# Keeping TensorE side pieces out of the round after a VectorE read of the side PSUM bank

## The chip, the cores and the metric

The kernel runs on one NeuronCore of one Trainium2 chip. The metric is the device time of one execution, in microseconds (us). The kernel before takes 10168.11 us, the median of three runs (10168.09 to 10171.36). The five engines are TensorE (PE, with its weight loads PEld), VectorE (DVE), ScalarE (ACT), GpSimd (POOL) and SyncE (SP, which here only issues DMAs).

## The reference

Two graph layers on 3327 nodes with 128 features; `adj` is a 0/1 matrix with about 0.24% ones and a full diagonal. Layer 0 is graph attention, layer 1 is a graph transformer in which the adjacency is added to the scores twice, once as "spatial" and once as "edge" encoding. Each layer is followed by a residual and a layer norm. Cut to what is computed:

```python
# layer 0
H = x @ W.T + b;  s = H @ a_s;  r = H @ a_r
e = leaky_relu(A * s + A * r.T, negative_slope=0.2)
att = softmax(where(A > 0, e, -9e15), axis=1)
x = layernorm(x + att @ H)
# layer 1: d = 128 "heads" of n = 3327 positions with h = 8 features
q, k, v = ((x @ Wx.T).reshape(d, n, h) for Wx in (Wq, Wk, Wv))
a = einsum('dnh,dmh->dnm', q, k) * d ** -0.5 + adj + adj
out = einsum('dnm,dmh->dnh', softmax(a, axis=2), v)
x = layernorm(x + out.reshape(n, h * d) @ Wo.T)
```

Nearly all the work is in layer 1: 128 score matrices of 3327 x 3327, each with an exponential per element. Because `q`, `k` and `v` are plain reshapes, a slice of 128 rows of layer 0's result feeds only a few of the 128 heads. So layer 1 can begin when the first row tile of layer 0 is ready, and the rest of layer 0 can be computed beside it.

## The kernel before, in words

The two layers run interleaved in one long loop, inside `special()`. (`shifted()` and `general()` are run only when a test of the data's range fails; here they don't run.)

**The main loop.** 32 groups `g` of four heads, in each 7 blocks `b` of 476 query columns, in each block 26 rounds `n`: 32 x 7 x 26 = 5824 rounds. Keys are cut into 26 tiles. In a round four score matmuls (L135) fill two PSUM tiles `scb` with the scores of two (key tile, half of the heads) pairs. Every third key tile is a "times" tile: ACT takes the exponential straight from PSUM (L1007), and POOL multiplies it by a factor made of the adjacency (L1008). For the other tiles DVE adds the adjacency out of PSUM into SBUF (L1010), and ACT takes the exponential a round later, for a whole tile (L843). The products of the exponentials with the values (L813, tile `av`) follow four rounds later. Rounds come in threes: two rounds with one times half and one added half each, then one round with two added halves. The last two rounds of a block, n = 24 and 25, are of the first kind, and so are the rounds 0 and 1 of the next block. There are two PSUM buffers `scb` for the added tiles and one for the times tiles, one PSUM bank for `av`, and one PSUM bank, `bank` (pool `sx_ps`, one buffer), for all the rest.

**The side work.** The remaining 25 row tiles of layer 0, and the last projection with its layer norm (`result`), are cut into pieces and run in the gaps of the loop. There are two rows of pieces. `main` holds, for each tile, 26 products of the attention (p, on TensorE, L450), then a chain that alternates between TensorE and DVE: transpose (`turn`), copy (`keep_turned`), and for each of 24 chunks of 128 columns a projection p (`project`, L373) that writes `bank`, and a DVE piece d that reads `bank`: for 16 chunks of q and k `halves` (two instructions, L386 and L389), for 8 chunks of v `values` (one copy, L408). `result` has such pairs too (`turn` at L472, `divided` at L481). `aside` holds the attention weights and counts: d pieces on DVE (L295, L313), m pieces on POOL (L304), x pieces (loads on SP).

**Who runs when.** `lane("p", n)` lets one p of `main` run in the rounds n = 3, 4, 7, 10, 13, 16, 19, 22, 24 and 25; `lane("d", n)` one d in 0, 4, 7, ..., 22, 24 and 25. A p is issued by `work_tensor` right after the round's score matmuls and ahead of its products. The d, from `main` if its head is a d and else from `aside`, is issued by `work` at the end of the round, behind the round's additions. The order is fixed when the program is built; every engine then works through its own list in order, held by semaphores. A p takes a new tile from the one-buffer pool `sx_ps`, so it waits until DVE is done with the piece before.

**The deadline.** 28 rounds before a group ends (L980) `finish_to` forces all pieces of `main` that the next group's rows still need, one after the other, into the program at that place. If they are done by then, it adds nothing.

Of the kernel before, what the change touches and what calls it, by code (L numbers as in the profile page):

```python
# [47 lines left out]
def kernel(  # L48
# [95 lines left out]
    def special():  # L144
        with ExitStack() as sx, tc.manual_schedule(engines=ALL):
# [468 lines left out]
            with ExitStack() as st:  # L614
# [8 lines left out]
                for p0, p1 in _cut(FP):  # L623
# [8 lines left out]
                loads, main, aside = layer0(  # L632
                    0, side=False, trow=trs[0], bank=lambda: pps.tile([P, 512], F32, tag="mm", name="mm")
                )
# [224 lines left out]
            def lane(kind, n):  # L859
                middle = n % 3 == 1 and 4 <= n < NR - 2  # L860
                if kind == "p":
                    return int(middle or n == 3 or n >= NR - 2)
                return int(middle or n == 0 or n >= NR - 2)
# [3 lines left out]
            main = []  # L867
            aside = []
# [21 lines left out]
            aside.append(("t", ("counts", 0)))  # L890
            results = [((needs[t] + 1) * total + LAG + 6, result(t)) for t in range(NT)]
            marks = {("P", q): 0 for q in range(len(CH))}
            side = {"main": [], "aside": aside, "since": {"main": 0, "aside": 0}}

            def head(row, now, force=False):

                while True:
                    if not side[row]:
                        if row == "aside":
                            return None  # L900
                        ahead = ("rows", reads[min(max(now, 0) // total + 2, NG - 1)]) in marks
                        if results and results[0][0] <= now and (ahead or not main):
                            side[row] = results.pop(0)[1]
                        elif main:
                            side[row] = main.pop(0)
                        else:
                            return None
                    kind, f = side[row][0]
                    if kind == "t":
                        marks[f] = now  # L910
                    elif kind == "w":
                        if not force and now - side["since"][row] < f:
                            return None
                    elif kind == "n":
                        if f[:2] not in marks or not force and now - marks[f[:2]] < f[2]:
                            return None
                    else:
                        return kind
                    side[row].pop(0)

            def run(row, now):
                side[row].pop(0)[1]()
                side["since"][row] = now

            def work_tensor(now, n):
                for _ in range(lane("p", n)):
                    if head("main", now) != "p":
                        break
                    run("main", now)

            def work(now, n):
                room, pool = lane("d", n), 1
                for row in ("main", "aside"):
                    while True:
                        kind = head(row, now)
                        if kind == "x":
                            pass
                        elif kind == "d" and room:
                            room -= 1
                        elif kind == "m" and pool:  # L940
                            pool -= 1
                        else:
                            break
                        run(row, now)
# [22 lines left out]
            for g in range(NG):  # L967
                k4, v4, _ = group
                for b in range(NBLK):
                    s = Block()  # L970
                    s.g, s.b, s.q4, s.k4, s.v4, s.left, s.e, added = g, b, queries[0], k4, v4, NT, {}, {}
                    for n, rnd in enumerate(rounds):
# [20 lines left out]
                        for i, h in rnd:  # L993
                            sc.append((pe if i in times else pd).tile([P, 2, 512], F32, name="scb"))
                            for t in range(2):
                                scores(sc[-1][: kr[i], t, :WB], s.k4, s.q4, i, kr[i], 2 * h + t, WB)
                        work_tensor(g * total + at, n)
                        for (i, h), z in zip(rnd, sc):
                            r = kr[i]
# [11 lines left out]
                        now = g * total + at  # L1011
# [14 lines left out]
                        while len(waiting) > LAG:  # L1026
                            products(*waiting.pop(0))
                        work(g * total + at, n)
            exp_late(NG * total + 2)
            while waiting:  # L1030
# [130 lines left out]
    def general():  # L1161
        with ExitStack() as gx:
# [168 lines left out]
            with ExitStack() as pc:  # L1331
                wp = pc.enter_context(tc.tile_pool(name="pc_w", bufs=3))
                ps = pc.enter_context(tc.tile_pool(name="pc_ps", bufs=4, space=bass.MemoryType.PSUM))
                for t in range(NT):
# [30 lines left out]
                    nc.scalar.dma_start(out[t * P : t * P + r, :], y[:r])  # L1365

    special()
    fine = nc.values_load(flag[0:1, 0:1])
    with tc.If(fine < 1):
# [41 lines left out]
```

## Time and profile before

| | |
|---|---|
| Median of three runs | 10168.11 us |
| The profiled execution: its own time | 10167.89 us |
| Its span, first to last instruction | 10166.1 us |
| Mean granted TensorE clock | 0.995 |
| Busy: PE / DVE / ACT / POOL | 98% / 92% / 98% / 91% |
| Rounds, and time per block of 26 rounds | 5824, 44.5 us |

Busy time is the union of an engine's instructions. In a row of a wait view the engine and line that waited stand first, then whom it waited for, the total in us, the number of times and the longest. In a timeline the columns are start, duration, engine, line, operation, tiles with their shapes and, in brackets, the engine's idle time before it and what ended it.

### The profile page before, as it was taken

The numbers are of one execution on the slowest core, as the hardware profiler recorded it, in microseconds if no ns is written. First come the engines' busy times: TensorE is split into PE (matmuls) and PEld (weight loads), VectorE is DVE, ScalarE is ACT, GpSimd is POOL, SyncE is SP. The second block draws the span as 40 slices with busy tenths as digits, with TensorE's granted clock in tenths as the row PEclk, the third lists the DMA queues.
The fourth block names the chain that finished last, engine by engine and source line by source line (L and its number), as shares of the span: only waits on it lengthen the run. The fifth ranks groups of instructions, "written<-read, shape, count | busy, mean of one in ns | idle before, by whom it ended". The sixth has DMA issues, their size and how long they took to land.

```text
span 10166.1 us, 212027 instructions
## 1 busy us (share of the span) xinstructions
PE 9930.1 (98%) x81993; PEld 3841.6 (38%) x81993; DVE 9374.0 (92%) x11597; ACT 9981.3 (98%) x8311; POOL 9215.6 (91%) x4395
## 2 busy tenths in 40 slices
PE   7999999999999999999999999999999999999998
PEld 3333333333333333333333333333333333333333
DVE  6999999999989999999999999999999999999887
ACT  6999999999999999999999999999999999999998
POOL 6999999999989999999999999999999999998887
PEclk8999999999999999999999999999999999999999
DMA  6655555555555555555555565555665555655554
GB/s 175 202 176 167 174 172 174 173 173 167 176 166 170 177 165 173 176 167 170 168 170 178 172 179 167 156 175 173 178 177 160 164 174 176 176 153 171 165 158 125
DMA packets 1183195, 1730.00 MB, mean 170 GB/s; under 512 B 131326, under 2 KB 1170783, under 8 KB 1177949
## 3 DMA queue, kind: packets, MB, share of 16 engines
q1 hardware_dynamic: 1180810, 1714.81, 56.8%
q8 instruction: 645, 10.57, 0.4%
q14 instruction: 377, 3.09, 0.1%
q10 hardware_dynamic: 1363, 1.53, 0.1%
HBM read 1611.93 MB, written 103.95 MB: 169 GB/s over the span
## 4 chain that ended last, share of the span: by engine, by line
PE 79%; ACT 10%; DVE 5%; POOL 2%; issue 2%; DMA 1%; SPq 0%; DVEq 0%; POOLq 0%; ACTq 0%
PE av L813 41%; PE scb L135 33%; ACT e L1007 5%; ACT e L843 5%; PE bank L224 4%; DVE e L1010 3%; POOL e L1008 2%; DVE o L822 1%; DMA at<-in_adjT_dram 0%; PE bank L472 0%; DMA k4b<-kT 0%; DMA at<-ftd 0%; POOL at L803 0%; DVE lo L389 0%; DVE ot L481 0%
## 5 line engine op out<-in xcount | busy, mean ns | idle before, releaser
L1008 POOL TENSOR_TENSOR e<-e,at 128x952 f32<-128x952 f32 x4032 | 8972.4, 2237 | 836.0 <-ACT e L1007 772.8
L1010 DVE TENSOR_TENSOR e<-scb,at 128x952 f32<-128x952 f32 (+1 forms) x7616 | 8420.3, 1145 | 671.2 <-PE scb L135 365.6
L843 ACT ACTIVATE e<-e 128x1904 f32<-128x1904 f32 (+2 forms) x4256 | 6885.4, 1624 | 14.7 <-DVE e L1010 14.3
L813 PE MATMUL av<-e,v4b 128*32 128x476 f32 x46592 | 5876.9, 572 | 40.2 <-DVE o L822 28.2
L135 PE MATMUL scb<-q4b,k4b 32*128 32x476 f32 (+1 forms) x23296 | 4338.4, 592 | 121.0 <-ACT e L1007 54.0
L135 PEld LDWEIGHTS scb<-q4b,k4b 32*128 32x128 f32 (+1 forms) x23296 | 2518.9, 295 | 4796.6 <-issue 2640.6
L1007 ACT ACTIVATE e<-scb 128x952 f32<-128x952 f32 x4032 | 3881.2, 963 | 88.0 <-PE scb L135 59.4
L813 PEld LDWEIGHTS av<-e,v4b 128*32 128x32 f32 x46592 | 1058.7, 108 | 1066.5 <-issue 621.5
L224 PE MATMUL bank<-hsb,w 128*32 128x129 f32 (+1 forms) x5200 | 277.9, 285 | 0.0
L313 DVE TENSOR_SCALAR_CACHE_REDUCE dump<-a 128x384 bf16<-128x384 f32 (+2 forms) x468 | 247.4, 529 | 0.6
L295 DVE TENSOR_SCALAR w<-trow,er 128x129 f32<-128x129 f32 x650 | 201.4, 339 | 13.1 <-DMA trow<-td 13.1
L304 POOL TENSOR_TENSOR w<-w,a 128x384 f32<-128x384 f32 (+3 forms) x225 | 207.0, 920 | 0.1
L224 PEld LDWEIGHTS bank<-hsb,w 128*32 128x32 f32 (+1 forms) x5200 | 102.4, 108 | 148.4 <-issue 148.4
L822 DVE COPY o<-av 128x476 f32<-128x476 f32 x224 | 145.9, 651 | 7.9 <-PE av L813 6.9
L389 DVE SCALAR_TENSOR_TENSOR lo<-bank,hi 128x128 fp32r<-128x128 f32 (+1 forms) x400 | 116.6, 292 | 13.9
L386 DVE TENSOR_SCALAR hi<-bank 128x128 fp32r<-128x128 f32 (+1 forms) x400 | 112.3, 281 | 0.0
L224 PE MATMUL bank<-wk,x1T 128*32 128x128 f32 x1600 | 85.2, 284 | 10.7 <-DVE lo L389 10.7
L224 PE MATMUL bank<-wq,x1T 128*32 128x128 f32 x1600 | 85.2, 284 | 9.0 <-DVE lo L389 9.0
L224 PE MATMUL bank<-wv,x1T 128*32 128x128 f32 x1600 | 85.4, 285 | 5.0 <-DVE vb L408 4.0
L224 PE MATMUL bank<-wo,ot 128*32 128x128 f32 (+1 forms) x1664 | 88.8, 290 | 0.4 <-DVE ot L481 0.4
L472 PE MATMUL bank<-identr,o 128*128 128x128 f32 (+1 forms) x234 | 54.6, 308 | 15.0 <-DMA o<-oT 8.1
L408 DVE COPY vb<-bank 128x128 f32<-128x128 f32 (+1 forms) x200 | 56.2, 281 | 3.5 <-PE bank L224 3.5
(110 smaller groups left out, 665.6 us busy)
## 6 DMA issues: line engine op xcount, KB each, us to landing
at<-in_adjT_dram SPq DMA_DIRECT2D x1736, 476.0 KB
at<-ftd SPq DMA_DIRECT2D x1953, 238.0 KB
q4b<-qT SPq DMA_DIRECT2D x1788, 29.8 KB
k4b<-kT SPq DMA_DIRECT2D x126, 415.9 KB
at<-in_adjT_dram SPq DMA_DIRECT2D x217, 208.2 KB
at<-in_adjT_dram SPq DMA_DIRECT2D x56, 714.0 KB
a<-in_adjT_dram SPq DMA_DIRECT2D x50, 504.0 KB
ftd<-at SPq DMA_DIRECT2D x63, 238.0 KB
```

Source lines behind the costliest of these rows:

```text
L135: nc.tensor.matmul(dst, k4[32 * j : 32 * j + H4, i::NT], q4[32 * j : 32 * j + H4, :nb], start=True, stop=stop,)
L224: nc.tensor.matmul(dst[c0:c1], w[:, c0:c1], mov, **kw)
L295: nc.vector.tensor_scalar(w, s["t"][:, :, :T3], e, None, op0=ALU.max)
L304: nc.gpsimd.tensor_tensor(w, w, s["a"][n][:, c0 - i0 : c1 - i0, :r], op=ALU.mult)
L313: nc.vector.tensor_scalar(z, a, float(k), None, op0=ALU.is_equal, op1=ALU.add, accum_out=even[:, t, at : at + 1])
L389: nc.vector.scalar_tensor_tensor(lo[:r, o : o + QW], s["b"][:r, :QW], scale, hi[:r, o : o + QW].bitcast(F32), op0=ALU.mult, op1=ALU.subtract,)
L813: nc.tensor.matmul(s.av[32 * j : 32 * j + 32, :], s.v4[:r, j, i * H1 : i * H1 + 32], e[:r, j, :], start=(s.left == NT - 1), stop=(s.left = ...
L822: nc.vector.tensor_copy(o4, s.av)
L843: nc.scalar.activation(e, e, AF.Exp, scale=2.0)
L1007: nc.scalar.activation(eh, z[:r, :, :WB], AF.Exp, scale=2.0)
L1008: nc.gpsimd.tensor_tensor(eh, eh, ah, op=ALU.mult)
L1010: nc.vector.tensor_tensor(eh, z[:r, :, :WB], ah, op=ALU.add)
```

## The change

A new entry `side["read"]` remembers the round in which the last d of `main` was run (one of `aside` does not count). `work_tensor` runs no p in the round after it. The pieces, the lanes and the deadlines are as they were; p pieces that lose their round come in a later one.

```diff
-            side = {"main": [], "aside": aside, "since": {"main": 0, "aside": 0}}
+            side = {"main": [], "aside": aside, "since": {"main": 0, "aside": 0}, "read": -2}
...
             def work_tensor(now, n):
-                for _ in range(lane("p", n)):
+
+                for _ in range(lane("p", n) if side["read"] != now - 1 else 0):
                     if head("main", now) != "p":
                         break
                     run("main", now)
...
                         elif kind == "d" and room:
                             room -= 1
+                            if row == "main":
+                                side["read"] = now
```

## The prediction

> **What bounds the kernel now.** First the busy shares and the costliest groups of the page:
>
> ```profile
> PE 9930.1 (98%) x81993; PEld 3841.6 (38%) x81993; DVE 9374.0 (92%) x11597; ACT 9981.3 (98%) x8311; POOL 9215.6 (91%) x4395
> ...
> L843 ACT ACTIVATE e<-e 128x1904 f32<-128x1904 f32 (+2 forms) x4256 | 6885.4, 1624 | 14.7 <-DVE e L1010 14.3
> ...
> L1007 ACT ACTIVATE e<-scb 128x952 f32<-128x952 f32 x4032 | 3881.2, 963 | 88.0 <-PE scb L135 59.4 <-DMA at<-in_adjT_dram 20.1 <-ACT e L843 0.6
> ```
>
> PE and ACT both show 98%. ACT is the one to believe: ahead of its 8288 exponentials it was idle for only 14.7 + 88.0 = 102.7 us, while PE stood waiting for ACT to empty the one times buffer 2245 times (1887.5 us of weight-load idle in the view of waits). The chain of work that ended last gives PE 79%, because ACT and PE hand a PSUM tile to and fro; I don't read it as slack on ACT. So a change can gain only where ACT is idle, and of that idle time 59.4 us in 102 places are put down to late score matmuls. Why were those late? The waits of PE name the side bank:
>
> ```profile
> PE bank L224 <- DVE lo L389: 20.2, 45, 0.6
> ...
> PE bank L472 <- DVE ot L481: 6.9, 13, 1.8
> PE bank L224 <- DVE vb L408: 4.0, 6, 1.2
> ```
>
> A side matmul waited 45 times for the second instruction of `halves`. Next I looked up where. In the timeline of rounds 24 and 25 of one block (the 55th):
>
> ```profile
> 2577.67 0.60 PE L135 MATMUL scb<-q4b,k4b 32*128 32x476 f32 x4
> 2577.96 0.28 DVE L386 TENSOR_SCALAR hi<-bank 128x128 fp32r<-128x128 f32 x1
> ...
> 2578.28 0.29 DVE L389 SCALAR_TENSOR_TENSOR lo<-bank,hi 128x128 fp32r<-128x128 f32 x1
> 2578.30 0.97 ACT L1007 ACTIVATE e<-scb 128x952 f32<-128x952 f32 x1
> ...
> 2578.71 0.42 PE L224 MATMUL bank<-wq,x1T 128*32 128x128 f32 x8 [0.45 <-DVE lo L389]
> ...
> 2578.93 1.01 PE L813 MATMUL av<-e,v4b 128*32 128x476 f32 x8
> ...
> 2579.87 0.61 PE L135 MATMUL scb<-q4b,k4b 32*128 32x476 f32 x4
> ...
> 2580.59 0.96 ACT L1007 ACTIVATE e<-scb 128x952 f32<-128x952 f32 x1 [0.44 <-PE scb L135]
> ```
>
> Round 24's d (L386, L389) comes behind DVE's additions and ends at 2578.57; round 25's p needs the same bank and starts at 2578.71, 0.45 us after PE became free. Behind it in PE's list stand the products and the next round's scores, so ACT waits 0.44 us. Two blocks of the loop earlier, round 24 has a p and no d of `main`:
>
> ```profile
> 2488.91 0.43 PE L224 MATMUL bank<-hsb,w 128*32 128x129 f32 x8
> ...
> 2489.01 0.97 ACT L1007 ACTIVATE e<-scb 128x952 f32<-128x952 f32 x1
> ...
> 2490.06 0.38 PEld L135 LDWEIGHTS scb<-q4b,k4b 32*128 32x128 f32 x4 [0.78 <-ACT e L1007]
> ...
> 2490.80 0.96 ACT L1007 ACTIVATE e<-scb 128x952 f32<-128x952 f32 x1
> ```
>
> The same side matmuls at the same place, and ACT runs on: from L1007 to L1007 1.79 us against 2.29. The half us is 0.44 idle and the overlap of two ACT instructions that is lost with it.
>
> [...]
>
> **The change part by part.** Reading the instruction order of both programs, a p directly follows a round with a d of `main` 81 times before, each in n = 25 after n = 24, and never after the change. (n = 3 follows a round without a d lane, n = 4 one without too, the others lie two rounds off.) What such a pair costs I took from the start times of L1007 in all blocks, round 25 to round 0; with a p in 25 but no d of `main` in 24 the median is 1.780 us, with no p in 25 it is 1.775 (so the p itself is hidden under ACT):
>
> - 45 pairs after `halves`: 2.285, so 0.505 each: 22.7 us.
> - 8 after `divided`: 2.263, 0.483 each: 3.9 us.
> - 20 after `values` (one copy, sooner done): 1.870, 0.090 each: 1.8 us.
> - 3 after the first two `divided`, 0.48 each; 2 transposes after layer 0's `scale`, 0.84 each; 3 after `keep_turned`, 0.05: 3.3 us.
>
> Together 31.7 us off. The gain is kept: the rest of the block, round 1 to the next round 24, has a median of 39.04 us after such a pair and 39.05 in blocks whose rounds 24 and 25 both hold products, so ACT neither catches up nor falls back later.
>
> Now where the pieces go. Round 25 holds 97 p's instead of 167. Of the 70 missing, 15 go to n = 3, 3 to n = 4, 36 to the middle rounds, 12 to n = 24, and 4 more are forced at the deadline. In n = 3 a p costs nothing (2.543 with and without); in the middle rounds 0 to 20 ns beside 2.53: 36 x 0.01 = 0.4 us. A p in n = 24 costs 0.122 (1.872 against 1.750): 12 x 0.122 = 1.5 us. In the rounds 25 that lose a p, DVE takes pieces of `aside` (147 instead of 77; 0.4 to 0.6 us, about a `halves`), and POOL 35 masks instead of 17, 0.92 us each. After the 12 windows of before with a mask in round 25 the next four rounds took the same median (7.805 us against 7.806), so I cost both at nothing; POOL's backlog is their cover, and if it were gone, 18 x 0.92 = 17 us. No instruction is added or taken away; loads and stores move with their pieces on SP's queue, past the `at` loads there, which are issued three stretches (some 13 us) ahead of their use and are their cover, and `main` ends in round 5802 instead of 5718, inside the loop's 5824.
>
> The deadline is the other cost. Before the change it forces 6 pairs at the end of group 0 and 2 at the end of group 1; after it, 8 and 4, all `values`, and none at later groups. A forced pair is a bare ping-pong between PE and DVE, one every 0.84 us, and PE's scores stand behind it:
>
> ```profile
> 380.96 0.43 PE L224 MATMUL bank<-wv,x1T 128*32 128x128 f32 x8 [0.41 <-DVE vb L408]
> 381.80 0.42 PE L224 MATMUL bank<-wv,x1T 128*32 128x128 f32 x8 [0.41 <-DVE vb L408]
> ```
>
> ACT was idle 5.51 us there and 1.75 at the second place. Four more pairs: 4 x 0.84 = 3.4 us. Beside it, the first stall made PE's clock drop to 0.50 from 383 to 393 us, and three rounds took 2.40, 2.55 and 2.37 instead of 1.87, 1.78 and 1.75: 1.9 us. The second stall, short, did not. With 4 pairs it may, and the first may last longer: between 0 and three times that, 5.6 us; I take 1.6. So 5.0 us in all. The new group's k and v loads come up to 1.7 us later, 28 and 12 rounds ahead of their use, and are hidden by these.
>
> Sum: 31.7 - 5.0 - 1.5 - 0.4 = 24.8 us off the profiled execution's 10167.9 (span 10166.1 plus 1.8 around it): 10143.1. The median of the runs lies 0.2 us higher, so 10143.
>
> **The rivals.**
>
> 1. The forecast: 10134 to 10148. For it: the cost of a pair is measured in the same round of the same loop, with and without. 0.72.
> 2. The deadline eats the gain: half clock after both stalls and for longer (5.6 us), POOL's masks or late `at` loads with a few us more; 10148 to 10158. For it: group 0 is the part where POOL and the DMAs are full anyway. 0.16.
> 3. The wait only changes its name: with the side bank out of the way, ACT's next score tile is held up by something else that is just as late (DVE's addition behind an `aside` piece), and half of the 31.7 us stay: 10159. Against it: blocks with an `aside` d in round 25 and no `main` d in 24 run at 1.780. 0.07.
> 4. Slower: POOL becomes the bound in rounds 24, 25, 0 and 1, each with a product of 2.24 us against 1.75 of ACT; more masks there, PE's products wait for POOL, and ACT behind them. It decides when some 76 blocks (those that lose a p after a d) lose 0.7 us each: 52 us, which swallows the gain and gives 10189. Against it: the windows with a mask above, and only 18 masks move in. 0.05.
>
> That the change does nothing is excluded by the order: 81 pairs before, none after.
>
> **How the numbers follow.** A measurement of this kernel tells about 0.2% (20 us) from no change; that line lies at 10147.8. Rival 1 is faster; 2 and 3 fall within 0.2%; 4 is slower, or nearly. Faster 0.72, same 0.23, slower 0.05. The range has to leave out no more than 2 in 10: from 10134 (no clock loss, all of the gain, and 3 us for the spread of runs) to 10157, which takes in most of rival 2.
>
> **What would show it.** In the profile after: PE's waits of L224 for L389 all but gone (45 before); ACT's idle before L1007 for L135 down from 59.4 us to some 35, in about 40 places; round 25 to 0 at 1.78 in every block; ACT idle of about 7.2 us at 385 us and 3.4 at 703 us, perhaps with a second drop of the clock. I'm wrong if L1007 still waits some 80 times under another releaser (rival 3), if POOL's products come late for L813 (4), or if the clock is low for more than some 20 us around the two deadlines (2).

## The result

The changed kernel takes 10147.32 us (median of 15 runs, 10146.3 to 10153.77), the kernel before 10168.09 in the same series (10165.18 to 10171.46). The ratio is 0.9981, 95% interval 0.9973 to 0.9989: 20.8 us faster, where 24.8 were forecast (10143, range 10134 to 10157).

The page and the view of waits of the changed kernel; three lines have been inserted, so ACT's exponential out of PSUM is now L1010 and DVE's addition L1013:

```profile
PE 9936.6 (98%) x81993; PEld 3855.0 (38%) x81993; DVE 9373.0 (92%) x11597; ACT 9978.5 (98%) x8311; POOL 9211.9 (91%) x4395
...
L843 ACT ACTIVATE e<-e 128x1904 f32<-128x1904 f32 (+2 forms) x4256 | 6886.4, 1624 | 16.3 <-DVE e L1013 15.5
...
L1010 ACT ACTIVATE e<-scb 128x952 f32<-128x952 f32 x4032 | 3882.0, 963 | 67.9 <-PE scb L135 37.7 <-DMA at<-in_adjT_dram 20.6 <-ACT e L843 0.6
```

The counts and durations are those of before. What moved is ACT's idle time ahead of its exponential: 67.9 us instead of 88.0, and within it the wait for late scores, 37.7 instead of 59.4. The waits of PE, and the one of ACT:

```profile
ACT e L1010 <- PE scb L135: 37.7, 41, 7.8
```

```profile
PE bank L224 <- DVE vb L408: 5.6, 10, 1.2
...
PE bank L472 <- DVE ot L481: 2.7, 2, 1.8
```

ACT waits in 41 places instead of 102, and PE's wait for L389 (20.2 us in 45 places before) is in the list no more. The wait for `vb` has grown, from 4.0 us in 6 places to 5.6 in 10: those are the forced pairs. Rounds 24 and 25 of the same block as before, in the timeline:

```profile
2578.08 0.60 PE L135 MATMUL scb<-q4b,k4b 32*128 32x476 f32 x4
2578.38 0.28 DVE L386 TENSOR_SCALAR hi<-bank 128x128 fp32r<-128x128 f32 x1
...
2578.61 1.01 PE L813 MATMUL av<-e,v4b 128*32 128x476 f32 x8
2578.69 0.29 DVE L389 SCALAR_TENSOR_TENSOR lo<-bank,hi 128x128 fp32r<-128x128 f32 x1
2578.71 0.96 ACT L1010 ACTIVATE e<-scb 128x952 f32<-128x952 f32 x1
...
2579.57 0.99 ACT L843 ACTIVATE e<-e 128x952 f32<-128x952 f32 x1
...
2579.73 0.70 PE L135 MATMUL scb<-q4b,k4b 32*128 32x476 f32 x4
...
2580.49 0.96 ACT L1010 ACTIVATE e<-scb 128x952 f32<-128x952 f32 x1
```

DVE reads `bank` as late as before (L389 ends at 2578.98), but the products no longer stand behind it: they start at 2578.61, 0.53 us after the start of the scores (1.26 us before). ACT goes from L1010 to L1010 in 1.78 us, where it took 2.29: the 0.44 us of idle time are gone, and L1010 starts 0.07 us before L843 ends (2580.56).

To see where the rest went I numbered the rounds in both traces by ACT's exponentials and added up the differences by place (after less before, us; the second trace of before is from the last of the experiments):

| place | forecast | against the trace of before | against a second trace of before |
|---|---|---|---|
| round 25 to 0, all blocks, clock apart | -31.7 | -31.0 | -30.6 |
| forced pairs at two deadlines | +3.4 | +4.3 | +4.5 |
| half clock behind them | +1.6 | -0.5 | +0.9 |
| ahead of the first round, and the tail | 0 | +0.8 | -0.1 |
| all other rounds | +1.9 | +5.5 | +3.2 |
| span | -24.8 | -20.9 | -22.1 |

### The profile page after: what moved, and what is told of

Read it like the earlier page. It is cut to its first block, busy times and chain, and to the rows that moved or that the text cites. A ratio compares the mean times of both kernels' runs of the same rounds, so it can differ in the third digit from the quotient of the medians.

```text
span 10145.2 us, 212048 instructions
## 1 busy us (share of the span) xinstructions
PE 9936.6 (98%) x81993; PEld 3855.0 (38%) x81993; DVE 9373.0 (92%) x11597; ACT 9978.5 (98%) x8311; POOL 9211.9 (91%) x4395
## 4 chain that ended last, share of the span: by engine, by line
PE 79%; ACT 12%; DVE 4%; issue 2%; POOL 2%; DMA 1%; SPq 0%; DVEq 0%; ACTq 0%; POOLq 0%
PE av L813 40%; PE scb L135 33%; ACT e L843 6%; ACT e L1010 6%; PE bank L224 4%; DVE e L1013 3%; POOL e L1011 2%; DVE o L822 1%; PE bank L472 0%; DMA at<-ftd 0%; DMA at<-in_adjT_dram 0%; POOL at L803 0%; PE mm L182 0%; PE pb L674 0%; DMA k4b<-kT 0%
## 5 line engine op out<-in xcount | busy, mean ns | idle before, releaser
L1013 DVE TENSOR_TENSOR e<-scb,at 128x952 f32<-128x952 f32 (+1 forms) x7616 | 8417.8, 1144 | 647.3 <-PE scb L135 333.0
L843 ACT ACTIVATE e<-e 128x1904 f32<-128x1904 f32 (+2 forms) x4256 | 6886.4, 1624 | 16.3 <-DVE e L1013 15.5
L813 PE MATMUL av<-e,v4b 128*32 128x476 f32 x46592 | 5872.4, 572 | 42.1 <-DVE o L822 27.8
L1010 ACT ACTIVATE e<-scb 128x952 f32<-128x952 f32 x4032 | 3882.0, 963 | 67.9 <-PE scb L135 37.7
L813 PEld LDWEIGHTS av<-e,v4b 128*32 128x32 f32 x46592 | 1056.6, 108 | 1068.5 <-issue 616.1
L822 DVE COPY o<-av 128x476 f32<-128x476 f32 x224 | 146.0, 652 | 7.5 <-PE av L813 6.7
L389 DVE SCALAR_TENSOR_TENSOR lo<-bank,hi 128x128 fp32r<-128x128 f32 (+1 forms) x400 | 116.6, 292 | 13.8
```

The lines of the kernel that those rows point to most:

```text
L389: nc.vector.scalar_tensor_tensor(lo[:r, o : o + QW], s["b"][:r, :QW], scale, hi[:r, o : o + QW].bitcast(F32), op0=ALU.mult, op1=ALU.subtract,)
L813: nc.tensor.matmul(s.av[32 * j : 32 * j + 32, :], s.v4[:r, j, i * H1 : i * H1 + 32], e[:r, j, :], start=(s.left == NT - 1), stop=(s.left = ...
L822: nc.vector.tensor_copy(o4, s.av)
L843: nc.scalar.activation(e, e, AF.Exp, scale=2.0)
L1010: nc.scalar.activation(eh, z[:r, :, :WB], AF.Exp, scale=2.0)
L1013: nc.vector.tensor_tensor(eh, z[:r, :, :WB], ah, op=ALU.add)
```

## The experiments

Beside the theory (PE's side piece waits for a late DVE read of the one side bank, in round 25 alone; the price is the deadline) stand the rivals of the prediction, and two of the kind "it isn't that wait": a p in round 25 is too much for PE, or the time goes with where pieces and DMAs happen to fall. An edit to `work_tensor` or `lane` is shown against the kernel that its text names.

**The deadline alone.** The rule in groups 0 and 1 only:

```diff
-                for _ in range(lane("p", n) if side["read"] != now - 1 else 0):
+                for _ in range(lane("p", n) if side["read"] != now - 1 or now >= 2 * total else 0):
```

> The rule is kept in groups 0 and 1 alone, so this is the deadline's price by itself: 8 and 4 forced pairs as in the changed kernel, and 76 of the 81 p-after-d rounds stay. Theory (the gain is the pairs in round 25, the deadline costs some 4.8 us): 5 pairs go (3 of halves, 1 of values, 1 of keep_turned), 1.7 us, against 4.8: about 10171, slower than before by 3. Rival (the deadline costs little and the missing part of the gain lies in the middle rounds): 10166 to 10168.

Measured: 10172.24 against 10167.12, 5.1 us slower (ratio 1.0005, 0.9996 to 1.0013, which alone is not clear of nothing; and in the trace the rounds behind both deadlines, where no rule acts any more, are 3.5 us longer, round 25 left out). In its trace the two places are plain. The waits of ACT from 378 to 390 us, the first deadline, and from 698 to 708 us, the second:

```profile
ACT e L1010 <- PE scb L135: 7.5, 1, 7.5
```

```profile
ACT e L1010 <- PE scb L135: 3.4, 1, 3.4
```

The same two places in the kernel before:

```profile
ACT e L1007 <- PE scb L135: 5.5, 1, 5.5
```

```profile
ACT e L1007 <- PE scb L135: 1.7, 1, 1.7
```

So the four forced pairs cost 2.0 and 1.7 us here. The deadline has a price of the forecast's size; the rival, that it has next to none, falls.

**Half a dose.** The rule in the even groups from 2 on:

```diff
-                for _ in range(lane("p", n) if side["read"] != now - 1 else 0):
+                for _ in range(lane("p", n) if side["read"] != now - 1 or now < 2 * total or now // total % 2 else 0):
```

> Half a dose: the rule in the even groups from 2 on. 43 of the 81 pairs stay, 38 go: 23 of halves, 7 of values, 4 of divided, 4 after layer 0's scale. Theory: 23 x 0.505 + 7 x 0.09 + 4 x 0.483 + 4 x 0.6 = 16.5 us off; one more forced pair (0.8) and 10 more p in round 24 (1.2): about 10153.6. Rival (the time of the whole moves with where DMAs and pieces happen to fall, not with the pairs): anywhere from 10147 to 10170, without proportion to the pairs that are gone.

Measured: 10155.12, ratio 0.9989 (0.9982 to 0.9995), 12.0 us faster where 14.5 were expected. PE's wait for L389 is there 22 times, which is the 22 `halves` pairs left:

```profile
PE bank L224 <- DVE lo L389: 9.8, 22, 0.5
```

The interval from round 25 to 0 gained 15.9 to 17.1 us (against the two traces of before), 16.5 expected. So the gain goes with the pairs. The other rounds have 1.0 to 3.4 us more, where 2.0 were expected; where the 2.5 us between 14.5 and 12.0 lie is not shown.

**The wait taken away in another way.** The kernel before, with all pieces in their old rounds; only in round 24 DVE does `main`'s d ahead of the addition:

```diff
                         work_tensor(g * total + at, n)
+                        early = n == NR - 2 and head("main", g * total + at) == "d"
+                        if early:
+                            run("main", g * total + at)
...
-                        work(g * total + at, n)
+                        work(g * total + at, n, early)
...
-            def work(now, n):
-                room, pool = lane("d", n), 1
+            def work(now, n, early):
+                room, pool = lane("d", n) - early, 1
```

> The kernel before, with all 81 pairs and every piece in its old round, but in round 24 main's d is put ahead of DVE's addition instead of behind it. Theory (the cost is only that DVE's read ends late): the wait of L224 for L389 goes, ACT's idle for L135 falls as in the changed kernel, no deadline is touched: 10168 - 31 = 10137, some us more if the addition, now about 0.6 us later, holds up the scores. Rival (a p in round 25 is too much for PE there, whoever reads): 10165 or more.

Measured: 10140.92, ratio 0.9975 (0.9965 to 0.9984): 26.2 us faster than before, where the change gained 20.8 in its own series; the intervals of the two overlap. The same two rounds of the same block:

```profile
2574.66 0.29 DVE L389 SCALAR_TENSOR_TENSOR lo<-bank,hi 128x128 fp32r<-128x128 f32 x1
...
2575.00 0.60 PE L135 MATMUL scb<-q4b,k4b 32*128 32x476 f32 x4
...
2575.53 0.42 PE L224 MATMUL bank<-wq,x1T 128*32 128x128 f32 x8
2575.64 0.97 ACT L1010 ACTIVATE e<-scb 128x952 f32<-128x952 f32 x1
...
2577.43 0.96 ACT L1010 ACTIVATE e<-scb 128x952 f32<-128x952 f32 x1
```

The side piece is in round 25 as before, starts 0.53 us after the start of the scores with no wait, and ACT takes 1.79 us. A p there costs nothing; that DVE's read ended late was all. Round 25 to 0 gained 31.1 to 32.3 us over all blocks, and no forced pair is added. The additions, 0.6 us later, held up nothing in rounds 24 and 25; whether the 3.0 us that this trace has in its other rounds from block 14 on are theirs was not tried.

**Both at once.** The change, and the d ahead of the addition (and `side["read"]` set there too):

```diff
                         if early:
                             run("main", g * total + at)
+                            side["read"] = g * total + at
```

> The change and, in round 24, main's d ahead of the addition, both at once. Theory (both remove the same wait): nothing is left for the second to gain, and the rule brings its deadline with it: 10140.9 + 4.8 + 1 = 10147, as the changed kernel (10147.3) and above the reordering alone (10140.9). Rival (an early d is worth something by itself, by freeing the bank or DVE sooner): 10135 or less.

Measured: 10146.69 (ratio 0.9979, 0.9971 to 0.9988), as the change alone. Both act on one wait, and with that gone the rule only costs.

**The rule without most of its deadlines.** From group 2 on:

```diff
-                for _ in range(lane("p", n) if side["read"] != now - 1 else 0):
+                for _ in range(lane("p", n) if side["read"] != now - 1 or now < 2 * total else 0):
```

> The rule from group 2 on alone: 6, 2 and 1 forced pairs at the first three deadlines instead of 8 and 4; 4 pairs after halves stay in groups 0 and 1. Theory (the deadlines cost the changed kernel some 4.8 us): 10147.3 - 4.8 + 0.8 for the new forced pair + 2.0 for the 4 pairs = 10145.3. Rival (the deadlines cost nothing): 10147.3 + 2.0 = 10149.3.

Measured: 10144.14 (ratio 0.9977, 0.9968 to 0.9986), 3.2 us under the change, though four pairs after `halves` are back; the kernel before was 1.1 us lower in this series than in that of the change, which leaves 2.1. Theory 10145.3, rival 10149.3. ACT's wait at the second deadline is 1.7 us again, and the clock is not halved there.

**No hurry at the deadlines.** The reordering alone, and in groups 0 and 1 one more d, in round 3 (`lane` is given `now` for it):

```diff
-                return int(middle or n == 0 or n >= NR - 2)
+                return int(middle or n == 0 or n >= NR - 2 or n == 3 and now < 2 * total)
...
+                        early = (n == NR - 2 or n == 3 and g < 2) and head("main", g * total + at) == "d"
```

> The reordering alone (no rule), and in groups 0 and 1 also a d in round 3, ahead of its addition, so that the chain runs one pair more per block there: 3 forced pairs at the first deadline instead of 6, none at the second instead of 2. Theory (a forced pair costs 0.84 us, and the half clock behind the first stall 1.9): 10140.9 - 5 x 0.84 - 0 to 1.9, + 1 for six d's in round 3: 10136 to 10138. Rival (the deadlines cost nothing): 10141 to 10142.

Measured: 10141.19 (ratio 0.9973, 0.9963 to 0.9984), no better than the reordering alone: a miss, and the number that the rival named. But the trace doesn't bear out the rival. The intervals into the two deadlines are 3.4 and 1.9 us shorter than with the reordering, as they should be; only 1.1 us are left at the end, since the first saving was lost again over the six blocks behind it (2.9 us ahead at the start of block 6, 0.4 behind at that of block 12). Of that, 2.1 us lie in the rounds 13 to 19 of block 6: PE waited 0.96 us for one of POOL's products there, and behind it the clock was at 0.50 from 416.0 to 419.4 us, in this trace alone; why that product was late is not shown. And in each of the blocks 9 to 13 the interval from round 4 to 6 is 0.44 to 0.77 us longer than with the reordering. There the new d shows: in block 10 the d of round 3 holds up DVE's copy of `av` (L822), for which the products of round 4 wait. First this trace, then the reordering alone:

```profile
579.16 1.01 PE L813 MATMUL av<-e,v4b 128*32 128x476 f32 x8 [0.64 <-DVE o L822]
```

```profile
579.38 1.00 PE L813 MATMUL av<-e,v4b 128*32 128x476 f32 x8 [0.19 <-DVE o L822]
```

So the forced pairs cost no less than was thought; but the new d's, priced at 1 us together, cost 2.9 in these five blocks.

**The pieces earlier.** The changed kernel with other lanes, no p in round 24, and in groups 0 and 1 alone more d's (`lane` is given `now` for it here too):

```diff
                 if kind == "p":
-                    return int(middle or n == 3 or n >= NR - 2)
-                return int(middle or n == 0 or n >= NR - 2)
+                    return int(3 <= n < NR - 2 and n % 3 != 2 or n == NR - 1)
+                return int(middle or n == 0 or n >= NR - 2 or now < 2 * total and n % 3 == 0 and n >= 6)
```

> The changed kernel with other lanes: no p in round 24, a p in the rounds 6, 9, ... 21 as well as 4, 7, ... 22 (in 25 as before), and in groups 0 and 1 alone a d in 6, 9, ... 21 too. No pair adjoins, none is forced at a deadline, 162 p leave round 24. Theory (rounds differ in what a p costs: 0.122 us in 24, next to nothing in the others): 31.7 for the pairs, 19.8 for round 24, about 8 for the deadline: 10168 - 59 = 10109. Rival (PE is as full as ACT, so a p costs the same wherever it goes): 10140 to 10147.

Measured: 10229.35, ratio 1.0062 (1.0049 to 1.0076): 62 us slower, a clear miss. Rounds 24 and 25 gained what was expected and more (25.3 and 33.6 us), but the intervals from the rounds 7, 10, 13, 16, 19 and 22 to the next but one lost 110 us together. A p in round 6 shows nothing in the interval from 6 to 7 (2.54 us with and without), and 0.24 us in the next one, from 7 to 9. DVE's wait for the scores, in the kernel before and here:

```profile
DVE e L1010 <- PE scb L135: 365.6, 1008, 1.6
```

```profile
DVE e L1013 <- PE scb L135: 615.0, 1900, 4.1
```

With 879 p's in the rounds 6, 9, ... 21 that is 110 / 879 = 0.125 us each, hardly other than the 0.122 in round 24; but the mean hides two prices. In the intervals from the rounds 10 to 22, one p in the round before costs 0.07 us (2.60 against 2.53 in the median), and a p in both rounds 0.21 (2.74). Of the rounds 3, 6, ... 24, round 3, from which I took "nothing", is the exception.

**None in 24, two in 4 and 13.** Against the kernel before:

```diff
-                    return int(middle or n == 3 or n >= NR - 2)
+                    return int(middle or n == 3 or n == NR - 1) + (n in (4, 13))
```

> The kernel before without a p in round 24, and with two in rounds 4 and 13 (n % 3 == 1) where the pieces allow it (some 170 second ones); 6 of the 81 pairs stay. Theory (a p costs 0.122 us in 24, 0.2 in the rounds 6 to 21 as the run with earlier pieces showed, and next to nothing in the rounds 4 to 22): 31.7 - 2 for the pairs and 19.8 for round 24 off, a second p at 0.02 to 0.1 each 3 to 17: 10122 to 10136. Rival (a second p in a round costs as much as one in 24 or more, since PE has no more slack): 10140 to 10160.

Measured: 10144.63 (ratio 0.9977, 0.9968 to 0.9987). It is a miss, and lies in the rival's range. Rounds 24 and 25 gained 25.0 and 29.7 us, but the rounds 7 and 16, next after those with a second p, lost 8.4 and 15.4, and 4 and 13 themselves 2.6 and 2.4: with some 160 second pieces 29 / 160 = 0.18 us each. The theory's upper end for a second p (0.1) was too low; PE's slack in this loop seems to take one piece in three rounds and not two, which agrees with the two prices of the run before.

**Before and after once more.** To see whether the 3 to 5 us spread over all other rounds are only the difference between two executions:

> The kernel before once more, to see how far two traces of one program differ. Against the first trace of before, those of the other kernels have some 3 us spread over all rounds (0.8 to 1 ns in each), and begin the loop 0 to 2 us later. Theory (that is the difference between two executions, not the change): this trace shows the same 3 us against the first one. Rival (the changed kernels pay it for their moved pieces): this trace repeats the first within 1 us outside the first 100 us.

> The changed kernel once more, in the same job. Theory: against the new trace of before, round 25 has 31 to 32 us less, the two deadlines 3 to 5 us more, and all the other rounds together are within 2 us. Rival: the other rounds again have 3 us or more over those of before.

Measured: one run each, 10169.07 and 10151.89. In the first 14 blocks the two traces of before stand 1.2 to 4.1 us apart, so a few us there can be scatter. From block 14 on the second repeats the first within 0.7 us; for those rounds the theory falls. The second trace of the changed kernel agrees with the first at round 25 (-30.2 us against the second of before) and at the deadlines (+5.2 with the clock), and its other rounds have more, not less: some 8.6 us, as the rival had it. Of these 5.3 lie in the last block (1.5 in the first trace). There the clock was low in this execution. The windows from 10074 to 10079 us, first of this trace and then of the first one of the changed kernel (the last number but two is the clock):

```profile
10074.00:10079.00 5.00, 4.91 (x34) 1.21 (x33) 3.80 (x5) 4.46 (x4) 3.74 (x2) 0.66 0.10 39
```

```profile
10074.00:10079.00 5.00, 4.80 (x39) 1.61 (x35) 4.75 (x11) 4.70 (x4) 3.61 (x3) 1.00 0.16 35
```

Three DVE pieces of the test of the data's range (the range test below; `within` twice and `least`) now fall into the rounds 24 and 25 of the block before and round 0 of this one, one after the other, where they had been three rounds apart. Here PE's weight loads wait for the additions, up to 2.0 us at a time in this trace and up to 1.4 in the other, and of the two only in this one the clock halved; the traces of the change with the reordering and of the rule from group 2 on have the low clock there too. Four of the 15 runs of the changed kernel are at 10151 to 10154, the others at 10146 to 10149, about that distance; that these are executions with the low clock was not shown.

## Why the prediction was right, and where it was off

- **Bound and place.** Right: ACT is the limit, and half a us of it was lost in round 25 behind a late DVE read. The reordering shows it best: same pieces, same rounds, no wait, no loss.
- **Size of the gain.** Right: 31.7 forecast, 30.2 to 31.0 measured. The price of a pair, read from the same round with and without it, carried over.
- **Deadline.** 5.0 forecast with the clock, 3.8 and 5.4 measured against the two traces of before. ACT's two waits became 7.8 and 3.7 us (7.2 and 3.4 forecast), the forced pairs cost 4.3 to 4.5 (3.4 forecast). The clock did drop behind the second stall too, as I had held possible; the windows of the changed kernel, 704 to 708 us:

```profile
704.00:708.00 4.00, 3.59 (x40) 1.18 (x32) 2.20 (x5) 1.85 (x2) 1.03 (x1) 0.60 0.50 133
```

  It cost 0.9 us there. Behind the first stall the low clock lasted 10.2 us in one trace of before and 6.8 in the changed kernel, so the longer stall had the shorter penalty; the sum of the clock's terms is -0.5 to +0.9, not 1.6.
- **Round 24.** 1.5 us were forecast for 12 more p's. Their price was there (1.87 us with one against 1.75), but the whole of round 24 came out at -0.1: of the blocks 14 to 212, seven had a long round 24 (2.00 to 2.22 us) before and three after (2.00). The longest one, at the range test, only moved, from block 214 (4.9 us) to block 221 (5.6 us).
- **All other rounds.** This is the term that was mis-sized: with round 24, 1.9 us were forecast, and 5.5 and 3.2 measured against the two traces of before. That is 3.6 of the 3.9 us by which the span missed the forecast against the first, but only 1.3 of 2.7 against the second. By place, against the first and the second:
  - The first 14 blocks: +1.3 and -1.0, no more than the two traces of before differ by there.
  - Blocks 14 to 212: +1.5 and +2.0, as much as was forecast. But two variants have as much or more from block 14 on, round 25 left out: the rule in groups 0 and 1 alone, which doesn't act there (3.5), and the reordering, in which no piece moved to another round (3.0). What these are stays open.
  - From block 213 on: +2.7 and +2.1, and +6.2 in the second trace of the changed kernel. Here the range test runs, in blocks 214 and 215 before and in blocks 221 to 223 after. The prediction saw that `main` ends later and put it at nothing, since it still ends inside the loop; but at its new place the test's DVE pieces crowd. In the two variants just named, where it kept its place, these blocks come to -0.6 and +0.6.
- **The rivals.** The wait did not come back under another name (ACT's places fell from 102 to 41), and POOL did not become the bound: the wait for its products ahead of PE's L813 is 344.8 us instead of 337.0, though 18 more masks stand in round 25. (The sum of that rival is a little off: 76 x 0.7 is 53 us, and on top of the forecast that is 10196, not 10189.)
- **Luck.** 10147.3 is inside the range by a wide margin, but inside the 10134 to 10148 of rival 1, the forecast, by only 0.7 us; five of the 15 runs lie above that. The terms that came out too small were in part made up for by the clock, which cost less than was thought.

## What to carry to other kernels

Here a side piece of 0.42 us on PE cost what stood behind it in PE's list: behind a late one the products started 1.26 us after the scores instead of 0.53, and ACT took 2.29 us instead of 1.78. So look for the piece that waits for a one-buffer tile, and at who reads that tile last. Reading earlier (0.6 us of DVE work moved ahead of an addition) was worth 26 us here, more than keeping the piece away (21), in the main because it slowed no chain that has a deadline: the forced pairs alone cost the change 4.3 to 4.5 us. And price a piece in the interval after it too: a place that looks free where the piece stands can pay one round later (a p in round 6: nothing up to round 7, 0.24 us from 7 to 9). That goes for pieces on the other engine too: the d put into round 3 cost 0.44 to 0.77 us behind a copy that its price had left out.

## What the runs showed of the hardware that was not expected

TensorE's clock was at 0.50 for 3.4 us, or twice or three times that, behind stalls of a few us, and not each time: behind the first deadline for 10.2, 6.8 and 3.4 us in traces with stalls of ACT of 5.5, 7.8 and 5.3 us (before, the changed kernel, before once more). Behind the second, the clock stayed at 1.00 with stalls of 1.7 and 3.4 us (before, and the rule in groups 0 and 1 alone), and fell to 0.50 behind stalls of 3.7 and 3.5 (the two traces of the changed kernel).

Two traces at the second deadline, each in two windows of 3.4 us: with the rule in groups 0 and 1 alone (a stall of 3.4 us), and the second one of the changed kernel (a stall of 3.5 us). The first busy time is PE's, and the clock is the last number but two:

```profile
698.40:701.80 3.40, 2.47 (x28) 0.92 (x20) 3.03 (x5) 2.99 (x3) 3.16 (x2) 1.00 0.78 288
701.80:705.20 3.40, 2.28 (x40) 1.16 (x44) 1.45 (x6) 0.38 (x1) 0.35 (x2) 1.00 0.02 7
```

```profile
701.90:705.30 3.40, 1.62 (x28) 0.77 (x28) 1.76 (x5) 0.26 (x1) 1.02 (x2) 1.00 0.03 13
705.30:708.70 3.40, 3.40 (x32) 1.23 (x32) 1.83 (x5) 2.09 (x3) 1.98 (x1) 0.50 0.67 188
```

The one stall is spread over both windows, with PE busy for 73% and 67% of them, and the clock was at 1.00 in both. The other lies mostly in the first, with PE busy for 48% of it, and in the second the clock was at 0.50. In the run without hurry the clock was at 0.50 from 416.0 us on, and PE had been busy for 72% of the 3.4 us ahead of it. So this is what was measured in three places; what decides whether a stall is followed by a low clock is not shown.
